# A recursive 2D filter by pairs of units: products read PSUM on VectorE, the quotient moves to GpSimd

## The chip, the cores and the metric

The kernel runs on one core of one Trainium2 chip. The metric is device time in microseconds for one launch, as the median of several runs. All data are float32.

## The reference, cut to what matters

The input `x` is (4, 512, 512, 16). Two residual layers follow each other, each on a group-normalised input. The first is a recursive filter in two dimensions that is applied by FFT; the second is a 3x3 cosine convolution. The change touches only how the filter of the first layer is built:

```python
a = jnp.pad(denumerator, ((0, 0), (0, 0), (1, 0), (1, 0)), constant_values=1.0)
b = jnp.pad(numerators, ((0, 0), (0, 0), (0, 0), (1, 0), (1, 0)), constant_values=0.0)
H_truncated = jnp.fft.rfft2(b, s=(l1, l2)) / jnp.fft.rfft2(a, s=(l1, l2))
h_truncated = jnp.fft.irfft2(H_truncated, s=(l1, l2))
H = jnp.fft.rfft2(h_truncated, s=(2 * l1, 2 * l2))
H_full = h0 + H[0]
```

`a` and `b` are 9x9 polynomials for each of 16 x 16 pairs of an input and an output channel. So for every pair of channels the kernel evaluates two complex polynomials A and B on a 512 x 257 grid, forms the complex quotient B / A = B conj(A) / |A|^2, and turns it into the spectrum of twice the size that the later convolution multiplies with.

## The kernel before, in words

Four phases run one after the other: `filter_phase` (the filter, from the weights alone, with the statistics of `x` slipped in beside it), `forward_phase` (transform of `x`), `conv_phase` (multiplication per frequency) and `last_phase` (inverse transform and second layer).

In `filter_phase` the work is a list of 1024 units: output channel j (16), column half h (2), input channel i (16, in pairs), row half kp (2). Two units that stand next to each other in the list, (i, i + 1), are a pair; there are 512. A unit covers 256 x 128 points of the grid, and passes through these steps:

- `polynomials` (L353): TensorE evaluates A and B of both units of a pair into four PSUM tiles `pab` of one bank each; in a tile the axes are partition, k (2), real or imaginary part (2), column (128). The PSUM pool `f_psab` has exactly four buffers.
- `evict` (L362, L365, L366): ScalarE (ACT) copies both tiles to SBUF (`ab`), then squares the real part of A into `sq` and the imaginary part back into PSUM.
- `square` (L370): VectorE (DVE) adds the squares to `dn`, which is |A|^2.
- `product` (L376, L377, L379): VectorE forms `m` = B A part by part and takes the reciprocal of `dn`; GpSimd (POOL) forms the crossed products `x`.
- `terms` (L383, L384): GpSimd adds and subtracts to the real and imaginary part of the numerator.
- `quotient` (L388): VectorE multiplies by the reciprocal into `sp`.
- `edge` (L393): for h = 0 ScalarE overwrites column 0 of `sp` with values `z` that `weights` has computed.
- `taps` and `placed` (L404, L415): TensorE transforms `sp` of a pair into two PSUM tiles `pg`, and ScalarE copies them into the staging tiles `st`. After the last unit of an (j, h), two `st` tiles of 4 MB each are stored in DRAM.

Beside these run three more things. `odds` (L456, L461) reads the finished part of an earlier channel back (`ev_in`), multiplies it on TensorE into `pt`, and ScalarE copies it to `ot`, which goes to DRAM; it is a generator, and each `next(rest)` copies the last `pt` and issues the matmuls of the next one. `weights` prepares the coefficients of the next channel once in 32 pairs. `quad` (L333, L335) prepares the left factors `u` of the polynomials for the next four input channels, once in four pairs; `pt` and the `pu` of `quad` share two PSUM buffers (`f_pst`). `image_stats` (L599) puts the statistics of `x` on VectorE; the scheduler places them, and `weights` and `quad` too.

All else keeps the order in which the code issues it on each of the four compute engines: the context manager `InOrder` ties each instruction to the one before it on its engine. The loop goes over units v. At v it issues `evict` and `square` for unit v, `product` for v - 1, `terms` and `quotient` for v - 2, `edge` for v - 3, and at every even v `polynomials` of the pair (v, v + 1) and `taps` and `placed` of the pair (v - 4, v - 3).

Of the kernel before, what the change touches and what calls it, by code (L numbers as in the profile page):

```python
# [40 lines left out]
F32 = mybir.dt.float32  # L41
AF = mybir.ActivationFunctionType
# [4 lines left out]
P = 128  # L47
# [154 lines left out]
def bc(ap, axis, shape):  # L202
    return ap.unsqueeze(axis).to_broadcast(shape)
# [45 lines left out]
def filter_phase(tc, cst, h0, num, den, g_d, beside):  # L249
    nc = tc.nc  # L250
    with ExitStack() as ctx:
# [3 lines left out]
        ew = ctx.enter_context(tc.tile_pool(name="f_ew", bufs=2))  # L255
# [14 lines left out]
        def weights(j):  # L270

            sa = wt.tile([18, C, 32], F32, name="sa")
            sb = wt.tile([18, C, 32], F32, name="sb")
            nc.gpsimd.dma_start(out=sa.rearrange("p i n -> p (i n)"), in_=cst["apad"])
            nc.gpsimd.memset(sb, 0.0)
            for t, src in ((sa, den), (sb, num)):
                for c in range(2):
                    nc.gpsimd.dma_start(  # L280
                        out=t[9 * c + 1 : 9 * c + 9, :, 9 * c + 1 : 9 * c + 9],
                        in_=src[:, j].rearrange("i p q -> p i q"),
                    )
            ha = sm.tile([18, C, 18], F32, name="ha")
            nc.gpsimd.tensor_mul(ha, sa[:, :, 0:18], bc(h0b[:, j :: C], 2, [18, C, 18]))
            nc.gpsimd.tensor_add(sb[:, :, 0:18], sb[:, :, 0:18], ha)


            v = sm.tile([18, 2, 4, C], F32, name="v")
            ev = sm.tile([18, 2, 2, C], F32, name="ev")  # L290
            od = sm.tile([18, 2, 2, C], F32, name="od")
            for n, t in enumerate((sa, sb)):
                for c in range(2):
                    q = 9 * c
                    nc.vector.reduce_sum(ev[:, c, n, :], t[:, :, q : q + 9 : 2], axis=AX.X)
# [24 lines left out]
            nc.vector.tensor_sub(z[:, :, 1, :], hz[:, :, 1, 0, :], hz[:, :, 0, 1, :])  # L320
            return sa, sb, z
# [19 lines left out]
        def polynomials(pair):  # L341

            for w in pair:
                w["pp"] = [ps_ab.tile([P, 2, 2, P], F32, name=f"pab{n}", tag="ab") for n in range(2)]
            for k in range(2):
                for w in pair:
                    k1 = (2 * w["kp"] + k) * P
                    for n in range(2):  # L350
                        at = 32 * (w["i"] % 4 ^ 2 * n)
                        q = slice(at, at + 18)
                        nc.tensor.matmul(  # L353
                            w["pp"][n][:, k].rearrange("p c n -> p (c n)"),
                            w["us"][n][q, k1 : k1 + P], e2[q, n, w["h"], :], start=True, stop=True,
                        )

        def evict(w):
            w["ab"] = [ew.tile([P, 2, 2, P], F32, name=f"ab{n}") for n in range(2)]
            pp = w.pop("pp")  # L360
            for n in range(2):
                nc.scalar.copy(w["ab"][n], pp[n])  # L362

            w["sq"], w["pa"] = ew.tile([P, 2, P], F32, name="sq"), pp[0]
            nc.scalar.activation(w["sq"], w["ab"][0][:, :, 0], AF.Square)  # L365
            nc.scalar.activation(pp[0][:, :, 1], w["ab"][0][:, :, 1], AF.Square)  # L366

        def square(w):
            w["dn"] = ew.tile([P, 2, P], F32, name="dn", bufs=3)
            nc.vector.tensor_add(w["dn"], w["sq"], w.pop("pa")[:, :, 1])  # L370

        def product(w):

            a, b = w["ab"]
            w["m"] = ew.tile([P, 2, 2, P], F32, name="m")
            nc.vector.tensor_mul(w["m"], b, a)  # L376
            nc.vector.reciprocal(w["dn"], w["dn"])  # L377
            w["x"] = ew.tile([P, 2, 2, P], F32, name="x", bufs=1)
            nc.gpsimd.tensor_mul(w["x"], b, a[:, :, ::-1])  # L379

        def terms(w):
            m, x = w["m"], w["x"]
            nc.gpsimd.tensor_add(m[:, :, 0], m[:, :, 0], m[:, :, 1])  # L383
            nc.gpsimd.tensor_sub(m[:, :, 1], x[:, :, 1], x[:, :, 0])  # L384

        def quotient(w):
            w["sp"] = ew.tile([P, 2, 2, P], F32, name="sp", bufs=4)
            nc.vector.tensor_mul(w["sp"], w["m"], bc(w["dn"], 2, [P, 2, 2, P]))  # L388

        def edge(w):  # L390
            if w["h"] == 0:
                kp = w["kp"]
                nc.scalar.copy(w["sp"][:, :, :, 0], w["z"][:, 2 * kp : 2 * kp + 2, :, w["i"]])  # L393
# [74 lines left out]
        def odds():  # L468

            for j in range(C):  # L470
# [4 lines left out]
        work = [dict(j=j, h=h, i=i, kp=kp)  # L475
                for j in range(C) for h in range(2) for i2 in range(0, C, 2) for kp in range(2)
                for i in (i2, i2 + 1)]
        done = [0]
        order = InOrder(tc, nc.tensor, nc.vector, nc.scalar, nc.gpsimd)
        rest = odds()  # L480
        polys = {0: weights(0)}
        us = quad(*polys[0][:2], 0)
        for v in range(len(work) + 3):
            with order:
                next(rest)
            if v % 64 == 32 and v < len(work) - 64:
                polys[v // 64 + 1] = weights(v // 64 + 1)
            first, second, third = (work[v - k] if 0 <= v - k < len(work) else None for k in (1, 2, 3))
            if third:
                with order:  # L490
                    edge(third)
            if v < len(work):
                w = work[v]
                if v % 8 == 0 and v:
                    us = ahead
                w["us"], w["z"] = us, polys[w["j"]][2]
                with order:
                    if v % 2 == 0:
                        pair = work[v : v + 2]
                        pair[1]["us"] = us  # L500
                        polynomials(pair)
            last = work[v - 4 : v - 2] if v % 2 == 0 and v >= 4 else None
            if last:
                if last[0]["i"] == 0 and last[0]["kp"] == 0:
                    st = [stp.tile([P, N, C], F32, name=f"st{a}", tag="st") for a in range(2)]
                with order:
                    pg = taps(last)
            if v < len(work):
                with order:
                    evict(work[v])  # L510
            if last:
                with order:
                    placed(last, st, pg)
                done[0] += 2
                for w in last:
                    w.clear()
            with order:
                if second:
                    terms(second)
                if first:  # L520
                    product(first)
                if second:
                    quotient(second)
                if v < len(work):
                    square(work[v])
            if v % 8 == 4 and v + 4 < len(work):
                g = (v + 4) // 8
                ahead = quad(*polys[g // 8][:2], g % 4)
            if v % 2:
                next(beside, None)  # L530
        done[0] += 8
        for _ in rest:
            pass
# [912 lines left out]
```

## Time and profile before

| | |
|---|---|
| median of 3 runs | 18399.56 us (18386.0 to 18413.88) |
| the profiled execution | 18378.82 us, its span 18377.0 us |
| mean granted TensorE clock | 0.939 |
| busy: PE, DVE, ACT, POOL | 88%, 61%, 52%, 57% of the span |
| first to last `reciprocal` of the filter (L377) | 36.6 to 5140.9 us |
| window 940 to 5140 us, busy: PE, DVE, ACT, POOL | 3617.8, 3329.4, 2513.1, 2680.0 of 4200 us |
| granted clock, 30 to 940 us and 940 to 5140 us | 0.74 and 0.89 |
| `pt` of the last channel, after the filter's units | to 5310 us |

PE is TensorE's matmul stream, PEld its weight loads. Busy is the time in which an engine executes something; a matmul's end is modelled, so a busy PE is not PE at its peak. The granted clock is the share of its full speed that TensorE was given. A row of the timeline has the start, the duration, the engine, the line of the kernel, the operation and the tiles that it writes and reads, and in brackets the idle time of the engine before it and what ended that.

### The profile page before, as it was taken

What the parts mean: (1) busy time and instruction counts of PE and PEld (TensorE: products, weight loads), DVE (VectorE), ACT (ScalarE), POOL (GpSimd) and SP (SyncE); (2) the same over time, 40 slices, a digit from 0 to 9 for tenths busy, and PEclk for the clock granted to TensorE, in tenths of its full rate; (3) what the DMA queues carried; (4) which work ended last, traced back from release to release, by engine and by line L of the source; (5) the groups of instructions that cost most, each with busy time, mean ns of one, the idle gap of its engine ahead of it and who ended that gap; (6) DMA issues with size and microseconds to landing.
All of it is one profiled execution on the core that took longest, in us unless ns stands there. A gap on an engine that the chain in (4) does not pass through costs nothing. (4 is left out here: it accounts for less than half of the span.)

```text
span 18377.0 us, 546088 instructions
## 1 busy us (share of the span) xinstructions
PE 16100.0 (88%) x233100; PEld 11615.5 (63%) x233100; DVE 11247.9 (61%) x23131; ACT 9599.6 (52%) x19919; POOL 10502.4 (57%) x10653
## 2 busy tenths in 40 slices
PE   7788888888889988888888888888888988988888
PEld 4444444444444467777777777777767776877777
DVE  8877777777833355555555555555555554246887
ACT  4556555555632255555555555555555554106788
POOL 5566666666621166666666666666666664026776
PEclk6888988888999999999999999999999999998999
DMA  4655555555676588888888888888888887795431
GB/s 123 201 162 165 162 165 162 164 163 161 167 221 184 167 319 320 318 321 324 316 321 318 319 325 323 325 325 323 323 323 314 325 320 289 257 324 192 160 129 69
DMA packets 2918877, 4543.47 MB, mean 247 GB/s; under 512 B 117634, under 2 KB 2086492, under 8 KB 2809694
## 3 DMA queue, kind: packets, MB, share of 16 engines
q1 hardware_dynamic: 2686254, 3768.39, 60.7%
q0 software_dynamic: 174896, 605.89, 8.7%
q10 hardware_dynamic: 55296, 134.24, 2.2%
q8 instruction: 1835, 30.06, 0.6%
q14 instruction: 596, 4.88, 0.1%
HBM read 3030.71 MB, written 1477.31 MB: 245 GB/s over the span
## 5 line engine op out<-in xcount | busy, mean ns | idle before, releaser
L838 PE MATMUL pg<-c_dg,g 64*128 64x128 f32 x32832 | 2836.9, 291 | 326.6 <-ACT gh L738 163.0
L854 PE MATMUL pm<-xe,gh 128*32 128x64 f32 x131328 | 2397.8, 222 | 587.8 <-issue 354.6
L854 PEld LDWEIGHTS pm<-xe,gh 128*32 128x32 f32 x131328 | 2011.9, 110 | 1165.3 <-issue 972.6
L838 PEld LDWEIGHTS pg<-c_dg,g 64*128 64x128 f32 x32832 | 2283.3, 190 | 670.4 <-issue 253.4
L456 PE MATMUL pt<-ev_in,c_todd 128*128 128x512 f32 x4096 | 2191.1, 681 | 350.4 <-ACT ot L461 323.9
L883 DVE TENSOR_TENSOR z<-zq,pz 128x256 f32<-128x256 f32 x2052 | 861.4, 420 | 2608.4 <-ACT zq L882 2531.1
L736 DVE COPY gh<-pg 128x512 f32<-128x512 f32 x2046 | 1410.1, 689 | 1312.1 <-PE pg L838 1308.2
L379 POOL TENSOR_TENSOR x<-ab,ab 128x512 f32<-128x512 f32 x1024 | 1561.1, 1524 | 1081.7 <-ACT ab L362 1029.0
L807 POOL TENSOR_TENSOR xu<-xe,c_late 128x256 f32<-128x256 f32 x2052 | 1389.5, 702 | 860.2 <-ACT xe L738 834.6
L377 DVE RECIPROCAL dn<-dn 128x256 f32<-128x256 f32 x1024 | 1781.8, 1740 | 0.0
L456 PEld LDWEIGHTS pt<-ev_in,c_todd 128*128 128x128 f32 x4096 | 792.4, 210 | 1483.1 <-issue 640.1
L738 ACT COPY yf<-pm 128x512 f32<-128x512 f32 x2046 | 1210.9, 592 | 924.0 <-PE pm L854 909.2
L362 ACT COPY ab<-pab 128x512 f32<-128x512 f32 x2048 | 1127.9, 617 | 858.7 <-PE pab L353 609.1
L818 ACT COPY xe<-xl 64x1024 f32<-64x1024 f32 x513 | 538.5, 1050 | 1872.5 <-POOL xl L809 1872.5
L738 ACT COPY gh<-pg 128x512 f32<-128x512 f32 x2058 | 1200.0, 583 | 398.4 <-PE pg L838 389.5
L875 PE MATMUL pz<-c_ident,yf 128*128 128x128 f32 x8208 | 1377.4, 291 | 30.3 <-issue 28.5
L404 PE MATMUL pg<-c_dinv,sp 64*128 64x128 f32 x16384 | 1192.7, 301 | 117.8 <-ACT sp L393 117.8
L404 PEld LDWEIGHTS pg<-c_dinv,sp 64*128 64x128 f32 x16384 | 1084.7, 209 | 313.2 <-PE pab L353 134.1
L376 DVE TENSOR_TENSOR m<-ab,ab 128x512 f32<-128x512 f32 x1024 | 1271.4, 1242 | 0.0
L809 POOL TENSOR_TENSOR xl<-xl,xu 128x1024 f32<-128x1024 f32 x513 | 1208.9, 2357 | 40.2
L383 POOL TENSOR_TENSOR m<-m 128x256 f32<-128x256 f32 x1024 | 747.0, 730 | 746.4 <-DVE m L376 746.2
L1289 PE MATMUL pc<-l_band,xn 128*128 128x160 f32 (+2 forms) x6144 | 1072.9, 333 | 53.7 <-DVE e_o L1344 53.5
(204 smaller groups left out, 31381.8 us busy)
## 6 DMA issues: line engine op xcount, KB each, us to landing
xe<-xf_d SPq DMA_DIRECT2D x1026, 1536.0 KB, 8.4
g<-g_d SPq DMA_DIRECT2D x511, 1024.0 KB, 9.8
g_d<-st SPq DMA_DIRECT2D x64, 4096.0 KB, 31.3
ev_in<-g_d SPq DMA_DIRECT2D x1024, 256.0 KB, 4.6
g_d<-ot SPq DMA_DIRECT2D x1024, 256.0 KB, 2.5
xf_d<-xe POOLq DMA_DIRECT2D x513, 448.0 KB, 8.3
xf_d<-xl POOLq DMA_DIRECT2D x513, 448.0 KB, 5.2
x_d<-xo SPq DMA_DIRECT2D x128, 1024.0 KB, 5.1
```

What stands on the lines that cost most here:

```text
L376: nc.vector.tensor_mul(w["m"], b, a)
L377: nc.vector.reciprocal(w["dn"], w["dn"])
L379: nc.gpsimd.tensor_mul(w["x"], b, a[:, :, ::-1])
L404: nc.tensor.matmul(pg[u][:, n, k].rearrange("p a x -> p (a x)"), w["sp"][q, k, c, :], dinv[q, 2 * kp + k, c, :], start=(c == 0), stop=(c = ...
L456: nc.tensor.matmul(pt, todd[:, c, kc, hh * P : hh * P + P], ev[:, kc, c], start=(kc == 0), stop=(kc == 1),)
L736: nc.vector.tensor_copy(dst, src)
L738: nc.scalar.copy(dst, src)
L807: nc.gpsimd.tensor_mul(u[:, :, h, c], xe[:, :, h, 1 - c], bc(late[:, 1 + c], 2, [P, F, 2]))
L809: nc.gpsimd.tensor_add(xl.rearrange("p f h c k -> p (f h c k)"), xl.rearrange("p f h c k -> p (f h c k)"), u.rearrange("p f h c k -> p (f ...
L838: nc.tensor.matmul(pg[c][:, j % 4], g[half, j], dg[half], start=True, stop=True)
L854: nc.tensor.matmul(pm[32 * q : 32 * q + 32, g % 8], gh[:, f].rearrange("p c j -> p (c j)"), xe[:, :, f].rearrange("p t h c k -> p t (h c k ...
L875: nc.tensor.transpose(pz[:, t % 4].rearrange("p v q x -> p (v q x)"), y[:, at].rearrange("p g x -> p (g x)"), ident)
```

## The change

The loop goes over pairs p instead of units. In an iteration `last` is the pair p - 2, `mid` is p - 1 and `new` is p. ScalarE copies only A to SBUF (`a`), and squares straight from PSUM. VectorE forms both kinds of products, `m` and `x`, out of B's PSUM tile, and adds `dn`; the two reciprocals of a pair come after all its products and after the `polynomials` and `evict` of the new pair in the code. GpSimd does `terms` and the `quotient`. `taps` of a pair stands before `polynomials` of the new one, and `next(rest)` is called at the start of an iteration and ahead of `evict`. Some SBUF buffers grow in number (`a`, `sq`, `m`, `dn` to 4, `x` to 3). The number of PSUM buffers is the same.

```diff
         def evict(w):
-            w["ab"] = [ew.tile([P, 2, 2, P], F32, name=f"ab{n}") for n in range(2)]
-            pp = w.pop("pp")
-            for n in range(2):
-                nc.scalar.copy(w["ab"][n], pp[n])
-
-            w["sq"], w["pa"] = ew.tile([P, 2, P], F32, name="sq"), pp[0]
-            nc.scalar.activation(w["sq"], w["ab"][0][:, :, 0], AF.Square)
-            nc.scalar.activation(pp[0][:, :, 1], w["ab"][0][:, :, 1], AF.Square)
-
-        def square(w):
-            w["dn"] = ew.tile([P, 2, P], F32, name="dn", bufs=3)
-            nc.vector.tensor_add(w["dn"], w["sq"], w.pop("pa")[:, :, 1])
-
-        def product(w):
-
-            a, b = w["ab"]
-            w["m"] = ew.tile([P, 2, 2, P], F32, name="m")
-            nc.vector.tensor_mul(w["m"], b, a)
-            nc.vector.reciprocal(w["dn"], w["dn"])
-            w["x"] = ew.tile([P, 2, 2, P], F32, name="x", bufs=1)
-            nc.gpsimd.tensor_mul(w["x"], b, a[:, :, ::-1])
+            pa, _ = w["pp"]
+            w["a"] = ew.tile([P, 2, 2, P], F32, name="a", bufs=4)
+            nc.scalar.copy(w["a"], pa)
+            w["sq"] = ew.tile([P, 2, P], F32, name="sq", bufs=4)
+            nc.scalar.activation(w["sq"], pa[:, :, 0], AF.Square)
+            nc.scalar.activation(pa[:, :, 1], pa[:, :, 1], AF.Square)
+
+        def products(w):
+
+            (pa, pb), a = w.pop("pp"), w["a"]
+            w["m"] = ew.tile([P, 2, 2, P], F32, name="m", bufs=4)
+            nc.vector.tensor_mul(w["m"], pb, a)
+            w["x"] = ew.tile([P, 2, 2, P], F32, name="x", bufs=3)
+            nc.vector.tensor_mul(w["x"], pb, a[:, :, ::-1])
+            w["dn"] = ew.tile([P, 2, P], F32, name="dn", bufs=4)
+            nc.vector.tensor_add(w["dn"], w["sq"], pa[:, :, 1])
...
         def quotient(w):
             w["sp"] = ew.tile([P, 2, 2, P], F32, name="sp", bufs=4)
-            nc.vector.tensor_mul(w["sp"], w["m"], bc(w["dn"], 2, [P, 2, 2, P]))
+            nc.gpsimd.tensor_mul(w["sp"], w["m"], bc(w["dn"], 2, [P, 2, 2, P]))
...
+        for p in range(n_pairs + 2):
+            new, mid, last = (work[2 * (p - k) : 2 * (p - k) + 2] if 0 <= p - k < n_pairs else [] for k in range(3))
             with order:
                 next(rest)
...
             if last:
...
+                    for w in last:
+                        edge(w)
+                    placed(last, st, taps(last))
...
             with order:
-                if second:
-                    terms(second)
-                if first:
-                    product(first)
-                if second:
-                    quotient(second)
-                if v < len(work):
-                    square(work[v])
...
+                for w in mid:
+                    products(w)
+                    terms(w)
+            if new:
...
+                with order:
+                    polynomials(new)
+            with order:
+                next(rest)
+                for w in new:
+                    evict(w)
+                for w in mid:
+                    nc.vector.reciprocal(w["dn"], w["dn"])
+                    quotient(w)
+            if p % 4 == 2 and p + 2 < n_pairs:
+                g = (p + 2) // 4
+                ahead = quad(*polys[g // 8][:2], g % 4)
+            next(beside, None)
```

In the changed kernel's own numbering the lines are: `a` L361, squares L363 and L364, `m` L370, `x` L372, `dn` L374, `terms` L378 and L379, `quotient` L383, `edge` L388, `taps` L399, `placed` L410, reciprocal L511, `pt` L451, `ot` L456.

More of the change, by code (lines that the diff above doesn't have):

```diff
@@ L482, in filter_phase @@
         us = quad(*polys[0][:2], 0)
-        for v in range(len(work) + 3):
+        n_pairs = len(work) // 2
+        for p in range(n_pairs + 2):
+            new, mid, last = (work[2 * (p - k) : 2 * (p - k) + 2] if 0 <= p - k < n_pairs else [] for k in range(3))
             with order:
                 next(rest)
[L486 to L491, printed above, removed]
-            if v < len(work):
[L493 to L502, printed above, removed]
+            if p % 32 == 16 and p < n_pairs - 32:
+                polys[p // 32 + 1] = weights(p // 32 + 1)
             if last:
@@ L506, in filter_phase @@
                 with order:
[L507 to L513, printed above, removed]
+                    for w in last:
+                        edge(w)
+                    placed(last, st, taps(last))
                 done[0] += 2
@@ L517, in filter_phase @@
             with order:
-                if second:
-                    terms(second)
-                if first:
-                    product(first)
-                if second:
-                    quotient(second)
-                if v < len(work):
-                    square(work[v])
-            if v % 8 == 4 and v + 4 < len(work):
-                g = (v + 4) // 8
+                for w in mid:
+                    products(w)
+                    terms(w)
+            if new:
+                if p % 4 == 0 and p:
+                    us = ahead
+                for w in new:
+                    w["us"], w["z"] = us, polys[w["j"]][2]
+                with order:
+                    polynomials(new)
+            with order:
+                next(rest)
+                for w in new:
+                    evict(w)
[4 more added lines that the diff above has]
+                g = (p + 2) // 4
                 ahead = quad(*polys[g // 8][:2], g % 4)
-            if v % 2:
-                next(beside, None)
+            next(beside, None)
         done[0] += 8
```

## The prediction, made before the changed kernel had run

> **What bounds the kernel now.** I read the windows first, to see which stretch the change can reach, then the timeline of an undisturbed pair of units, engine by engine, then what disturbs pairs, then rows for operations that are new. The filter runs from 30 to 5140 us of an 18377.0 us span; what follows keeps its order, so a gain there moves the end one for one. VectorE near 5130 us (start, us, engine, line):
>
> ```profile
> 5127.60 0.40 DVE L370 TENSOR_TENSOR dn<-sq,pab 128x256 f32<-128x256 f32 x1
> 5127.93 1.43 DVE L376 TENSOR_TENSOR m<-ab,ab 128x512 f32<-128x512 f32 x1
> 5129.28 1.74 DVE L377 RECIPROCAL dn<-dn 128x256 f32<-128x256 f32 x1
> 5130.95 0.62 DVE L388 TENSOR_TENSOR sp<-m,dn 128x512 f32<-128x512 f32 x1
> 5131.49 0.40 DVE L370 TENSOR_TENSOR dn<-sq,pab 128x256 f32<-128x256 f32 x1
> ```
>
> No idle time stands behind a row: from `dn` to the next `dn` is 3.89, a unit, and the starts of L377, every second one, give 7.76 for a pair. Records overlap their successors by 0.08, so the starts give each step's share: `dn` 0.33, `m` 1.35, reciprocal 1.67, `sp` 0.54. PE in the same pair:
>
> ```profile
> 5127.23 3.83 PE L456 MATMUL pt<-ev_in,c_todd 128*128 128x512 f32 x8
> 5130.99 0.71 PE L353 MATMUL pab<-c_e,u 18*128 18x256 f32 x6
> 5131.95 1.13 PE L353 MATMUL pab<-c_e,u 18*128 18x256 f32 x10 [0.25 <-DVE dn L370]
> 5133.00 2.06 PE L404 MATMUL pg<-c_dinv,sp 64*128 64x128 f32 x32
> ```
>
> It idles only 0.25 of the 7.76. And with `quad`, once in four pairs:
>
> ```profile
> 2413.19 1.06 PE L333 MATMUL pu<-c_e,sa 18*32 18x512 f32 x8
> 2415.03 1.06 PE L333 MATMUL pu<-c_e,sb 18*32 18x512 f32 x8 [0.78 <-ACT ot L461]
> 2416.02 3.70 PE L456 MATMUL pt<-ev_in,c_todd 128*128 128x512 f32 x8
> 2419.65 1.15 PE L353 MATMUL pab<-c_e,u 18*128 18x256 f32 x16
> 2420.73 2.06 PE L404 MATMUL pg<-c_dinv,sp 64*128 64x128 f32 x32
> 2422.71 3.83 PE L456 MATMUL pt<-ev_in,c_todd 128*128 128x512 f32 x8
> ```
>
> `quad` costs PE 2.83 (2413.19 to 2416.02). Then `pab` comes in one piece, 1.08, and the pair takes 6.69. With `pt` at 3.75 and `pg` at 1.98, PE's own work is 6.81: VectorE is the bound by less than 1 us.
>
> The starts of L377 give all pairs. The first 80, with the image statistics beside them, take 904 us: 76 at 10.3 and four near 31. The other 431 take 4196: 282 at 7.76, 27 at 29.1, 122 between, so 404 undisturbed ones of 8.44 on average. Two windows show what disturbs (columns: PE, PEld, DVE, ACT, POOL busy, clock, DMA share, GB/s):
>
> ```profile
> 2060.00:2080.00 20.00, 8.49 (x53) 5.15 (x54) 4.54 (x6) 5.75 (x17) 3.98 (x4) 0.67 0.99 267
> 2448.00:2450.00 2.00, 2.00 (x7) 0.79 (x4) 1.88 (x3) 1.76 (x5) 1.84 (x3) 0.58 0.44 131
> ```
>
> In the first the store of two `st` tiles fills the DMA engines and all engines stand. The second lies behind the next `quad`: after 74 of 107 quads the trace has the granted clock halved, mostly for 3.41 us, in which PE loses 1.71.
>
> **The change part by part**, for a pair.
>
> *Products (L370, L372 of the changed kernel).* VectorE loses two `m` (2 x 1.35) and two `sp` (2 x 0.54) and gets four 128x512 products with an operand in PSUM. The nearest row is the cosine of the last phase, PSUM times SBUF in the same shape (ns, least/median/most); below it the old `m`:
>
> ```profile
> L1307 DVE TENSOR_TENSOR e_y<-pc,l_rin x256: 627/684/701, 16647.6 to 18359.8; 128x512 f32<-128x512 f32 x128
> ```
> ```profile
> L376 DVE TENSOR_TENSOR m<-ab,ab x1024: 672/1418/1873, 35.7 to 5139.6; 128x512 f32<-128x512 f32 x171
> ```
>
> Bounds 0.63 and 1.42; I take 0.68, pitch 0.60, for its operands lie as the new ones do, and `m` shows what slows it: at its least it takes 0.67, and 1.43 where GpSimd's `x` (1.64) runs beside it, while `dn`, PSUM and SBUF, stays at 0.40 beside that `x`. VectorE: 4 x 0.60 + 2 x 0.33 + 2 x 1.67 = 6.40 (7.02 with no overlap) against 7.76. The Trainium skill (GPSIMD Engine Reference, Specifications) says that GpSimd shares its SBUF interfaces with VectorE, with contention when VectorE reads two SBUF inputs. The trace's `m` agrees; by that rule none of VectorE's new work is slowed.
>
> *Quotient on GpSimd (L383).* It loses two `x` and gets two 128x512 products. Bounds: 1.06 (L1330, two broadcast inputs) and 1.64; I take 1.28 (L1335, same shape, 1.26 to 1.31). GpSimd: 4 x 0.73 + 2 x 1.28 = 5.5, at worst 6.2, under PE's 6.81. The second `sp` is ready 1.3 after its reciprocal; `pg` (L399) asks for it an iteration later.
>
> *B is not evicted.* The order of instructions has 1,024 ACT copies fewer, 0.48 each by their starts. ACT has idle time, so that saves nothing; its squares read PSUM instead of SBUF, 0.38 to 0.49 by the rows, nothing either way. What goes is cover. All four `pab` buffers belong to one pair, and B's two now wait for a VectorE product. ACT's starts in the pair:
>
> ```profile
> 5128.39 0.63 ACT L461 COPY ot<-pt 128x512 f32<-128x512 f32 x1
> 5128.87 1.14 ACT L362 COPY ab<-pab 128x512 f32<-128x512 f32 x2
> 5129.82 0.49 ACT L365 ACTIVATE sq<-ab 128x256 f32<-128x256 f32 x1
> 5130.14 0.45 ACT L366 ACTIVATE pab<-ab 128x256 f32<-128x256 f32 x1
> ```
>
> `ot` 0.48, a copy 0.48, squares 0.32. PE now runs `pt`, `pg` of pair p-2, `pab` of p, `pt`. Laid out from `pab` at 0: `pt` from 1.08 to 2.95, next `pt` to 4.83, `pg` to 6.81. ACT first ends four `st` copies and `ot`, so `a` starts at 1.8; the reciprocals of p-1 end at 2.0, the products run from 2.5 to 5.6, and `pab` of p+1 wants them at 6.81: 1.2 to spare. Were they later, `pt` and `pg` would queue behind `pab`. For h = 0 `pg` also waits for `edge`, on ACT behind `ot`. That loop is `st` 1.06, `ot` 0.48, evict 2 x 1.12, `ot` 0.48, edges 0.24, `pg` 1.98, and five hand-overs of 0.08 (`m` ends at 5129.36, GpSimd starts at 5129.44): 6.88. So PE becomes the bound, at 6.81 to 6.88.
>
> *Reciprocals last.* They lie beside `pab` and evict, as laid out. The queues of SP, ACT and GpSimd issue the same DMAs in nearly the same order. The statistics end some 16 units later in VectorE's order, at no cost.
>
> *quad and storms.* `quad` will wait for an `ot` behind evict; by the layout its halves start 1.84 apart, as now, so 2.83 again, but on the engine that bounds. The store of `st` is DMA time: nothing saved.
>
> **Sum.** Four later pairs take 4 x 6.83 + 2.83 + (74/107) x 1.71 = 31.3, or 7.83 each, and 0.13 for `weights` (4 us a channel, 13 channels, 404 pairs): 7.96 against 8.44, x 404 = 194 us. First 80: VectorE gives 1.36, or 0.74 without overlap, with PE partly in the way at a clock of 0.74; I take 0.9 x 76 = 68. Together 262. The profiled execution took 18378.82, 1.82 around its span, and would go to 18117; the median of the runs is 20.7 above it, 18399.56 - 262 = 18138, say 18140.
>
> **The rivals.** *The same (10%): a serial loop through ACT.* With whole durations instead of starts the h = 0 loop is 1.21 + 0.63 + 2 x 1.5 + 0.63 + 0.50 + 2.06 + 0.4 = 8.4. Half of the pairs then cost 8.4 + 0.71 + 0.30 + 0.13 = 9.5, or +222; the other half saves 97, the first pairs 68: 18457 at the full price, 18400 at three quarters of it, which I take. Against it: ACT's rows do overlap. *Slower (9%): the products cost what `m` did.* VectorE then takes 4 x 1.35 + 0.66 + 3.34 = 9.40 and hides `quad`: +1.09 x 404 and +1.6 x 76, 18960. It decides from a pitch of 1.08: 4 x 1.08 + 4.0 = 8.31 = 8.44 - 0.13. For it: part of `m`'s 1.42 might not be GpSimd's doing; against it L1307. *Slower (6%): the clock.* If PE's pauses before `pab` halve the clock in each pair, 6.83 + 1.71 + 0.71 + 0.13 = 9.38, +380, 18780. Against it: from 2400 to 2500 us no stretch of 3.41 us in which PE was busy for over 90% has a halved clock behind it, and PE will idle less. The Trainium skill (TensorE: Matmul & The Clock Gate, A second HAM failure mode: psum-queue depth-cycling) tells of a kernel whose clock swings because PE pauses as it cycles through PSUM; the trace has that only behind quads and storms.
>
> **How the numbers follow.** Forecast 75%, rivals 25%. No change means within 0.2%, 37 us, about what a measurement of this kernel can tell. Low end: no halved clock, 7.52 + 0.13, 0.79 x 404 = 319, and 1.4 x 76 = 106: 17974, say 17970. High end: PE keeps its 0.25 of waits, each quad halves the clock, the first pairs give nothing: (4 x 7.08 + 2.83 + 1.71)/4 + 0.13 = 8.34, 40 us, 18360; to take in most of the serial loop, 18420. The other two, 15%, lie beyond. Faster 0.75, same 0.09, slower 0.16.
>
> **What would show it.** Right: L370 and L372 near 0.68, L383 near 1.28, pairs by the starts of L511 at 6.8 to 7.0, PE all but never idle between quads. Wrong: products over 1.08; `pab` waiting for `dn` or `x` for over 0.5 a pair; `pg` waiting for `edge`; a mean clock under 0.85 from 1000 us to the filter's end.

## The result, and the profile after

The changed kernel takes 18162.74 us (median of 4 runs, 18159.94 to 18203.43) against 18398.17 for the kernel before beside it: 235 us less, a ratio of 0.9877 with a 95% interval of 0.986 to 0.9894. The forecast was 18140 in a range of 17970 to 18420. Its profiled execution has a span of 18157.8 us against 18377.0, and the 219 us between them lie in the filter: its reciprocals run from 39.9 to 4923.3 us; in the kernel before they ran from 36.6 to 5140.9.

The timeline of VectorE in an undisturbed pair and the start of the next (start, us, engine, line, operation, tiles, shapes, count, then idle time before the row and who ended it; `...` stands for rows left out, here and in the code):

```profile
2616.32 0.69 DVE L370 TENSOR_TENSOR m<-pab,a 128x512 f32<-128x512 f32 x1 [0.80 <-ACT a L361]
2616.93 0.68 DVE L372 TENSOR_TENSOR x<-pab,a 128x512 f32<-128x512 f32 x1
2617.52 0.41 DVE L374 TENSOR_TENSOR dn<-sq,pab 128x256 f32<-128x256 f32 x1
2617.85 0.68 DVE L370 TENSOR_TENSOR m<-pab,a 128x512 f32<-128x512 f32 x1
...
2619.38 3.35 DVE L511 RECIPROCAL dn<-dn 128x256 f32<-128x256 f32 x2
2623.11 0.69 DVE L370 TENSOR_TENSOR m<-pab,a 128x512 f32<-128x512 f32 x1 [0.37 <-ACT a L361]
```

A pair now takes 2623.11 - 2616.32 = 6.79 us instead of 7.76, and VectorE, which had no idle time, waits 0.37 in it for `a`. TensorE, which idled 0.25 us in the pair before, is now the one without a gap:

```profile
2618.75 2.06 PE L399 MATMUL pg<-c_dinv,sp 64*128 64x128 f32 x32
2620.74 1.15 PE L353 MATMUL pab<-c_e,u 18*128 18x256 f32 x16
2621.81 3.70 PE L451 MATMUL pt<-ev_in,c_todd 128*128 128x512 f32 x8
2625.54 2.06 PE L399 MATMUL pg<-c_dinv,sp 64*128 64x128 f32 x32
...
2630.52 1.06 PE L333 MATMUL pu<-c_e,sa 18*32 18x512 f32 x8
2632.24 1.06 PE L333 MATMUL pu<-c_e,sb 18*32 18x512 f32 x8 [0.66 <-ACT ot L456]
```

`quad`, the last two rows, waits as it did: its second half stands until `ot` is copied, 0.66 here against 0.78 before. The new operations, each by its own line (ns, least/median/most):

```profile
L370 DVE TENSOR_TENSOR m<-pab,a x1024: 615/683/694, 34.9 to 4920.1; 128x512 f32<-128x512 f32 x171
...
L372 DVE TENSOR_TENSOR x<-pab,a x1024: 665/679/686, 35.5 to 4920.7; 128x512 f32<-128x512 f32 x171
...
L383 POOL TENSOR_TENSOR sp<-m,dn x1024: 1257/1272/1319, 41.7 to 4925.2; 128x512 f32<-128x512 f32 x171
```

The first 80 pairs, with the statistics beside them, are another matter: 904 us before, 897 after. There VectorE and ScalarE hold each other up. From the waits of the changed kernel between 380 and 930 us (who waited <- for whom: total us, times, longest):

```profile
DVE stats L585 <- DMA xs<-in_x: 98.3, 32, 10.5
...
ACT pab L364 <- DVE stats L585: 66.0, 32, 8.1
...
ACT a L361 <- DVE stats L585: 49.1, 15, 7.2
...
ACT st L410 <- DVE stats L585: 22.8, 3, 9.0
```

The same rows of the kernel before, in the same window:

```profile
DVE stats L599 <- DMA xs<-in_x: 49.7, 18, 6.5
...
ACT u L335 <- DVE stats L599: 6.1, 1, 6.1
...
ACT st L415 <- DVE stats L599: 4.1, 2, 2.4
```

So ScalarE stood 138 us for the statistics, where it had stood 10, and VectorE's wait for the loads of `xs` doubled.

Nothing in `evict` reads the statistics. The timeline of both engines in the changed kernel shows what ScalarE stands at:

```profile
600.85 1.06 DVE L585 BATCH_NORM_STATS2 stats<-xs 128x6 f32<-128x128 f32 x5 [1.09 <-DMA xs<-in_x]
...
602.15 3.36 DVE L511 RECIPROCAL dn<-dn 128x256 f32<-128x256 f32 x2
...
604.04 0.39 ACT L363 ACTIVATE sq<-pab 128x256 f32<-128x256 f32 x1
...
605.43 1.19 DVE L585 BATCH_NORM_STATS2 stats<-xs 128x6 f32<-128x128 f32 x6
...
606.08 0.33 ACTq L573 DMA_DIRECT2D xs<-in_x  x1
...
606.46 0.37 ACT L364 ACTIVATE pab<-pab 128x256 f32<-128x256 f32 x1 [2.02 <-DVE stats L585]
```

ScalarE has done `sq` at 604.43 and comes to the load of the next `xs` tile in its own queue (L573). There are two `xs` buffers, and the load may not go out before VectorE has finished the statistics of the tile that holds its buffer; these stand behind both reciprocals in VectorE's order. So ScalarE's square of the same unit, and the evict after it, come 2.02 later, and VectorE's products with them.

### The profile page after: what moved, and what is told of

Read it like the earlier page. It is cut to its first block, busy times and chain, and to the rows that moved or that the text cites. A ratio compares the mean times of both kernels' runs of the same rounds, so it can differ in the third digit from the quotient of the medians.

```text
span 18157.8 us, 546802 instructions
## 1 busy us (share of the span) xinstructions
PE 15836.8 (87%) x233100; PEld 11492.6 (63%) x233100; DVE 10706.4 (59%) x23131; ACT 9126.2 (50%) x18895; POOL 10230.0 (56%) x10653
## 5 line engine op out<-in xcount | busy, mean ns | idle before, releaser
L451 PE MATMUL pt<-ev_in,c_todd 128*128 128x512 f32 x4096 | 2110.2, 658 | 93.0 <-ACT ot L456 70.6
L511 DVE RECIPROCAL dn<-dn 128x256 f32<-128x256 f32 x1024 | 1717.7, 1717 | 0.0
L383 POOL TENSOR_TENSOR sp<-m,dn 128x512 f32<-128x512 f32 x1024 | 1302.6, 1272 | 643.5 <-DVE dn L511 593.8
L451 PEld LDWEIGHTS pt<-ev_in,c_todd 128*128 128x128 f32 x4096 | 782.0, 204 | 1166.1 <-issue 779.2
L410 ACT COPY st<-pg 128x256 f32<-128x256 f32 x2048 | 620.1, 390 | 1736.3 <-PE pg L399 1272.6
L399 PEld LDWEIGHTS pg<-c_dinv,sp 64*128 64x128 f32 x16384 | 1059.9, 205 | 663.4 <-ACT sp L388 352.6
L378 POOL TENSOR_TENSOR m<-m 128x256 f32<-128x256 f32 x1024 | 746.1, 729 | 1244.8 <-DVE m L370 1244.2
L399 PE MATMUL pg<-c_dinv,sp 64*128 64x128 f32 x16384 | 1162.4, 296 | 215.6 <-ACT sp L388 178.6
L370 DVE TENSOR_TENSOR m<-pab,a 128x512 f32<-128x512 f32 x1024 | 698.3, 682 | 1084.2 <-ACT a L361 1051.1
```

The costliest lines, as they stand in the source:

```text
L383: nc.gpsimd.tensor_mul(w["sp"], w["m"], bc(w["dn"], 2, [P, 2, 2, P]))
L399: nc.tensor.matmul(pg[u][:, n, k].rearrange("p a x -> p (a x)"), w["sp"][q, k, c, :], dinv[q, 2 * kp + k, c, :], start=(c == 0), stop=(c = ...
L451: nc.tensor.matmul(pt, todd[:, c, kc, hh * P : hh * P + P], ev[:, kc, c], start=(kc == 0), stop=(kc == 1),)
```

## The experiments

There were three groups of four; the kernel before, run beside each, took 18398.24, 18350.69 and 18337.83 us, so kernels of different groups are compared by their ratio to it (0.0010 is 18 us). Most intervals are 0.0009 to 0.0017 to each side. Stages come from the traces, by the starts of the reciprocals: the sums over the first 80 pairs and over the other 431. A storm is the three pairs around a store of `st`. "h = 0" and "h = 1" are the median pair of each half of a channel without `quad` and clear of the storms and of `weights` (12 of each 32 pairs); "quad" is the mean pair with `quad` that is clear of the same.

| kernel | ratio to before | first 80 | other 431 | h = 0 | h = 1 | quad |
|---|---|---|---|---|---|---|
| before | 1 | 904 | 4196 | 7.76 | 7.76 | 9.69 |
| changed | 0.9877 | 897 | 3985 | 6.79 | 6.69 | 10.40 |
| `xs` on SyncE | 0.9843 | 791 | 4031 | 6.79 | 6.69 | 10.40 |
| statistics in order | 0.9768 | 701 | 4015 | 6.79 | 6.69 | 10.36 |
| the same in before | 0.9945 | 775 | 4228 | 7.77 | 7.77 | 9.81 |
| half of `pt` | 0.9811 | 878 | 3895 | 6.79 | 6.27 | 10.06 |
| half of `pt`, edge on GpSimd | 0.9718 | 760 | 3833 | 6.27 | 6.27 | 9.86 |
| two SBUF inputs | 1.0032 | 932 | 4239 | 8.09 | 8.09 | 9.38 |
| quotient on VectorE | 0.9983 | 907 | 4146 | 7.97 | 7.97 | 8.24 |
| reciprocals by unit | 0.9910 | 908 | 4038 | 6.79 | 6.98 | 10.01 |
| units | 0.9962 | 897 | 4116 | 7.17 | 7.08 | 10.38 |
| statistics in order, `pu` in `pg`'s buffers | 0.9723 | 687 | 3921 | 6.79 | 6.69 | 8.89 |
| the same and edge on GpSimd | 0.9678 | 666 | 3851 | 6.69 | 6.69 | 8.88 |

**The first 80 pairs.** The theory is the loop just shown. The first test takes the loads off ScalarE's queue.

```diff
-        nc.scalar.dma_start(out=t, in_=x[b, ...])
+        nc.sync.dma_start(out=t, in_=x[b, ...])
```

> The changed kernel, with the loads of the image statistics (xs, L573) issued by SyncE instead of ScalarE. Theory (a loop through two queues holds the first 80 pairs): ScalarE stands before each load until VectorE has finished the statistics of the tile that held the buffer, and these lie behind reciprocals in VectorE's order; then evict is late and VectorE waits for a. With the loads off ScalarE's queue its waits for stats go (by the waits of 380 to 930 us: 66 us at L364, 49 at L361, 23 at L410), and the first 80 pairs fall from 897 us to 830 to 860: the whole by 40 to 65 us, to 18100 to 18120. Rival (VectorE's own work, 6.40 + 2.95 a pair, or the loads' transfer bounds this stretch): 880 us or more, the whole within 15 us of the changed kernel. The other 431 pairs stay at 3985 by both.

18107.52 us (18088.91 to 18126.98, 5 runs), 0.9843 (0.983 to 0.9857): 55 under the changed kernel's median (by the ratios 0.0034, give or take 0.0022), and the trace's 511 pairs add up to 60 less (4881.7 to 4822.0). In its list of waits from 380 to 930 us no row has ScalarE waiting for `stats` any more; the rows that stand there now for the evict's copy and for the loads are

```profile
ACT a L361 <- PE pab L353: 45.8, 25, 5.9
...
DVE stats L585 <- DMA xs<-in_x: 19.0, 3, 16.4
```

So most loads also come in time (19.0 instead of 98.3). The first 80 pairs fell by more than expected, 106, and the other 431 rose by 46, where none was expected: of pairs over 20 us there are two fewer in the first part and two more in the second, so part of this is where the line between the parts happens to lie, and the sum is the sounder number. The Trainium skill (DMA: Bandwidth & Descriptors, Issuing engines are not separate DMA queues) says that DMAs run on the same engines whoever issues them, and that spreading them only saves the issuing time, usually small. Here ScalarE lost more to a load than its issue: an issue takes 0.33 us of its queue, 43 for all 128 loads, and the waits in front of the issues were 138 us in this window alone. The edit takes both off ScalarE, and this run does not tell apart what each was worth. SyncE now does the waiting, 207.7 us for `stats` in the same window, with the stores of `ot` and the loads of `ev_in` behind it; that cost less.

The second test leaves the loads on ScalarE, and ties the statistics to the loop, two in each pair, instead of letting them run ahead.

```diff
-            next(beside, None)
+            with order:
+                next(beside, None)
```

> The changed kernel, with the image statistics held to the order of the loop: two bn_stats in every pair over all 511 pairs, instead of about 12 in each of the first 80. Theory (VectorE has slack once PE is the bound): the first 80 pairs cost what the later ones do on average (3984.5 / 431 = 9.25 us, so 740 instead of 897), and the later ones pay only what the 0.47 us of statistics a pair does not find idle on VectorE, 0.05 to 0.3 us: +20 to +120. Together 40 to 140 us less; I take 110, 18050. Rival (VectorE is as full as it was): the work costs the same wherever it stands, 404 x 0.47 = 190 more against 157 less, so 18160 to 18200.

17980.56 us (17947.61 to 17996.32, 4 runs), 0.9768 (0.9755 to 0.9782): 182 under the changed kernel, more than the 40 to 140. The first 80 pairs cost 701 (740 expected), the others 31 more (20 to 120 expected). The median pair stays at 6.79, though the first of every four in h = 0 rises to 6.95, with this on VectorE:

```profile
2575.85 0.42 DVE L586 BATCH_NORM_STATS2 stats<-xs 128x6 f32<-128x128 f32 x2
...
2576.18 0.67 DVE L370 TENSOR_TENSOR m<-pab,a 128x512 f32<-128x512 f32 x1
```

In the pair shown the statistics stand where VectorE waited 0.37 for `a`, and no wait is left there. The control was the same edit in the kernel before.

> The same edit in the kernel before, as a control. Theory (there VectorE was the bound, with no slack in 300 of the 404 undisturbed pairs): first 80 pairs 125 us less (9.74 x 80 = 779 instead of 904), the others 300 x 0.47 = 140 more: within 40 us of the kernel before, 18360 to 18440. Rival (the early stretch loses its time to ScalarE's queue in both kernels, so that spreading the statistics helps both alike): 40 to 140 us less than before here too.

18301.83 us (18277.26 to 18331.3, 5 runs), 0.9945 (0.9933 to 0.9958): 96 us less, so this expectation missed, and the rival's number came. Not for the rival's reason, though: the kernel before hardly lost time to ScalarE's queue (the 10 us above), and its first 80 pairs fell by 129, about the theory's 125. It was the later pairs, which were to pay 140 on a full VectorE, that paid only 32, and their median stays at 7.77. VectorE in this run, with GpSimd's `x` (POOL, L379) put in:

```profile
2598.42 1.65 POOL L379 TENSOR_TENSOR x<-ab,ab 128x512 f32<-128x512 f32 x1
...
2599.18 1.43 DVE L376 TENSOR_TENSOR m<-ab,ab 128x512 f32<-128x512 f32 x1
2600.53 1.74 DVE L377 RECIPROCAL dn<-dn 128x256 f32<-128x256 f32 x1
...
2602.31 1.64 POOL L379 TENSOR_TENSOR x<-ab,ab 128x512 f32<-128x512 f32 x1
...
2603.07 0.47 DVE L600 BATCH_NORM_STATS2 stats<-xs 128x6 f32<-128x128 f32 x2
2603.46 1.03 DVE L376 TENSOR_TENSOR m<-ab,ab 128x512 f32<-128x512 f32 x1
...
2606.94 1.43 DVE L376 TENSOR_TENSOR m<-ab,ab 128x512 f32<-128x512 f32 x1
```

From the first `m` to the last it is 7.76, as without statistics. Behind them `m` starts 0.39 later and takes 1.03 instead of 1.43. Both times it ends 0.54 after GpSimd's `x` does (2600.61 and 2600.07, 2604.49 and 2603.95), and that is the rule: in the kernel before, of 749 `m` between 960 and 4800 us that start while `x` runs, 98% end 0.546 to 0.554 after it, whenever they started. So `m` stood until `x` was done and then ran: 0.89 of its 1.43 was a wait. A VectorE without a gap did have room: it was busy waiting, inside `m`. Moving the statistics was worth 96 us in the kernel before and 182 after the change; the other 86 are there only with the change. By the traces it is 69, nearly all of it in the first 80 pairs (197 less against 129).

**What bounds an undisturbed pair now.** Half of each `pt` is left out, which takes 1.87 us a pair from TensorE.

```diff
-                        for kc in range(2):
+                        for kc in range(1):
                             nc.tensor.matmul(
...
-                                start=(kc == 0), stop=(kc == 1),
+                                start=True, stop=True,
                             )
```

> The changed kernel, with the second of the two accumulating matmuls of every pt left out (its output is not the reference's): PE loses 4 x 0.47 = 1.87 us a pair, from 6.81 to 4.94. Theory (PE bounds the undisturbed pair): the median pair falls from 6.79 us to what VectorE takes, 6.40 to 6.55, and quad hides, so that the 404 later pairs fall from 7.86 on average to 6.6 to 7.0: 350 to 500 us less, 17650 to 17800. Rival 1 (VectorE bounds it, at 6.8 with waits between): the median stays at 6.75 to 6.8 and only quads gain, 250 us at most. Rival 2 (the edge loop through ScalarE bounds pairs of h = 0): those stay at 6.79 and the pairs of h = 1 fall to 6.4 to 6.55.

18050.97 us (18041.04 to 18075.78, 4 runs), 0.9811 (0.9797 to 0.9824): 112 less, not 350 to 500. By the pairs it is rival 2: those of h = 1 fall from 6.69 to 6.27 (the rival had 6.4 to 6.55), those of h = 0 stay at 6.79. TensorE in one of these:

```profile
2611.57 1.98 PE L451 MATMUL pt<-ev_in,c_todd 128*128 128x512 f32 x4
2615.30 2.06 PE L399 MATMUL pg<-c_dinv,sp 64*128 64x128 f32 x32 [1.75 <-ACT sp L388]
```

TensorE is done early, and `pg` then waits for `edge`, which stands in ScalarE's order behind `st`, `ot`, both evicts and `ot`. Nor did `quad` hide, as the theory had it (10.06 against 10.40): its second `pu` still waits for `ot`, a median of 1.08 us instead of 0.66, and the granted clock is halved behind 69 of 107 quads instead of 43. The next run takes `edge` out of that loop, on top of the same edit: GpSimd does it, behind its quotient.

```diff
-                nc.scalar.copy(w["sp"][:, :, :, 0], w["z"][...])
+                nc.gpsimd.tensor_copy(w["sp"][:, :, :, 0], w["z"][...])
...
                 with order:
-                    for w in last:
-                        edge(w)
                     placed(last, st, taps(last))
...
                     quotient(w)
+                    edge(w)
```

> As the run with half of each pt left out (0.9811 of before; its pairs of h = 0 took 6.79 us, those of h = 1 took 6.3), with edge on GpSimd right behind the quotient instead of on ScalarE behind ot; the output is not the reference's. Theory (the loop st, ot, evict, ot, edge, pg holds the pairs of h = 0): they fall to 6.3 to 6.4 as well, 60 to 90 us less, 0.976 to 0.978 of before. Rival (ScalarE's list or GpSimd's holds them): they stay at 6.75 to 6.8, 0.980 to 0.982.

17817.74 us (17797.79 to 17830.57, 4 runs), 0.9718 (0.9703 to 0.9732). All undisturbed pairs are at 6.27, and no row of VectorE in them has idle time before it, so the loop through `edge` is what held h = 0, and VectorE holds both halves now. The gain is larger than expected because the first 80 pairs fall too, by 118; the later ones fall by 62, as expected. Why the first ones do was not tested by itself.

So three limits lie close together: VectorE at 6.27, TensorE at 6.69, the loop through `edge` at 6.79.

**The parts of the change.** First the operands: A twice from SBUF, where the changed kernel reads B from PSUM.

```diff
-            nc.vector.tensor_mul(w["m"], pb, a)
+            nc.vector.tensor_mul(w["m"], a, a)
...
-            nc.vector.tensor_mul(w["x"], pb, a[:, :, ::-1])
+            nc.vector.tensor_mul(w["x"], a, a[:, :, ::-1])
```

> The changed kernel, but the four products of a pair read A twice from SBUF (a times a) instead of B in PSUM and A in SBUF; the output is not the reference's. Theory (two SBUF inputs on VectorE are slowed while GpSimd works, as m was before): L370 and L372 rise from 0.68 us to 1.0 to 1.42, VectorE's pair from 6.40 to 4 x (0.92 to 1.34) + 4.0 = 7.7 to 9.4; the median pair goes from 6.79 to at least 7.6, the whole up by 300 to 700 us, 18460 to 18860. Rival (m's 1.42 was its own): both stay at 0.68, and the whole within 30 us of the changed kernel.

18417.98 us (18394.11 to 18426.14, 7 runs), 1.0032 (1.0021 to 1.0044): slower than the kernel before, and 0.0155 over the changed kernel, 285 us, just under the expected 300. VectorE and GpSimd in one stretch:

```profile
2601.30 0.62 DVE L370 TENSOR_TENSOR m<-a 128x512 f32<-128x512 f32 x1
2601.85 1.75 DVE L372 TENSOR_TENSOR x<-a 128x512 f32<-128x512 f32 x1
...
2603.00 1.18 POOL L378 TENSOR_TENSOR m<-m 128x256 f32<-128x256 f32 x1
```

A product of the same shape takes 0.62 where it starts with GpSimd idle and 1.75 where it starts in the middle of a GpSimd operation (medians: 0.71 for L370, under the 1.0 that was expected at least, and 1.21 for L372); GpSimd's L378 takes 1.18 instead of 0.73 (the median of the changed kernel). The pair is 8.09. The Trainium skill (SBUF — State Buffer, Who interferes with whom) says that a VectorE instruction with two SBUF inputs contends with a GpSimd instruction that reads SBUF, and one with a single SBUF input doesn't. Both halves agree: 0.68 with B in PSUM, 1.75 without in the row shown.

The quotient, put back on VectorE:

```diff
-            nc.gpsimd.tensor_mul(w["sp"], w["m"], bc(w["dn"], ...))
+            nc.vector.tensor_mul(w["sp"], w["m"], bc(w["dn"], ...))
```

> The changed kernel with the quotient back on VectorE (nothing else moved). Theory: VectorE gets 2 x 0.54 more a pair, 6.40 + 1.08 = 7.48, and bounds the pair again: the median pair goes from 6.79 us to 7.3 to 7.5, some 300 undisturbed pairs without quad pay 0.5 to 0.7 each, and the others little: 120 to 230 us more than the changed kernel, 18280 to 18390. Rival (VectorE has that much room, so the quotient's move brought nothing): median at 6.8, within 30 us of the changed kernel.

18313.13 us (18299.91 to 18345.69, 10 runs), 0.9983 (0.9974 to 0.9992): 0.0106 over the changed kernel, 195 us, as expected. The pair is longer than expected, 7.97:

```profile
2604.91 1.75 DVE L511 RECIPROCAL dn<-dn 128x256 f32<-128x256 f32 x1
2606.76 0.69 DVE L383 TENSOR_TENSOR sp<-m,dn 128x512 f32<-128x512 f32 x1
2607.37 1.75 DVE L511 RECIPROCAL dn<-dn 128x256 f32<-128x256 f32 x1
2609.22 0.69 DVE L383 TENSOR_TENSOR sp<-m,dn 128x512 f32<-128x512 f32 x1
```

Here `sp` reads the reciprocal right in front of it and starts 1.85 after that one's start, not 1.67 as behind another unit's reciprocal in the kernel before. Part of it comes back where `quad` is hidden again (8.24).

The place of the reciprocals: each right behind its unit's `dn` (moved from the end of the pair into `products`).

```diff
             nc.vector.tensor_add(w["dn"], w["sq"], pa[:, :, 1])
+            nc.vector.reciprocal(w["dn"], w["dn"])
...
-                    nc.vector.reciprocal(w["dn"], w["dn"])
                     quotient(w)
```

> The changed kernel with each reciprocal behind its own unit's dn, instead of both at the end of the pair. Theory (the last place lets both units' products give their PSUM back before the reciprocals): the second unit's dn comes 1.67 us later, pab of the next pair was to have 1.2 to spare, so PE waits 0.3 to 0.5 a pair: the median pair goes from 6.79 to 7.1 to 7.3, the whole up by 100 to 200 us, 18260 to 18360. Rival (the order within VectorE does not matter): within 30 us of the changed kernel, pairs at 6.8.

18181.37 us (18168.46 to 18214.95, 4 runs), 0.9910 (0.9893 to 0.9926): 0.0033 over the changed kernel, 60 us give or take 43, less than the 100 to 200 expected. VectorE and TensorE:

```profile
2601.12 1.75 DVE L375 RECIPROCAL dn<-dn 128x256 f32<-128x256 f32 x1
...
2602.79 0.63 DVE L370 TENSOR_TENSOR m<-pab,a 128x512 f32<-128x512 f32 x1
...
2603.79 1.73 PE L353 MATMUL pab<-c_e,u 18*128 18x256 f32 x16
```

The mechanism is there: the second unit's products start behind the reciprocal, and `pab` is stretched from 1.15 to 1.73 as it waits for them. But it strikes only some of the pairs: the median is 7.19 over all 431 later ones, 6.79 over the undisturbed ones of h = 0 and 6.98 over those of h = 1, which lie on both sides of that number.

Last, the new operations in the old loop over single units (products ahead of `pab`, reciprocal and quotient behind `evict`, one unit an iteration; the diff to the kernel before, cut to the loop):

```diff
+            if first:
+                with order:
+                    products(first)
+                    terms(first)
...
-                if second:
-                    terms(second)
                 if first:
-                    product(first)
-                if second:
-                    quotient(second)
-                if v < len(work):
-                    square(work[v])
+                    nc.vector.reciprocal(first["dn"], first["dn"])
+                    quotient(first)
```

> The new operations in the old loop over single units: products of B in PSUM by VectorE, quotient by GpSimd, B not evicted, but one unit an iteration, its products ahead of pab, its reciprocal and quotient behind evict. Theory (the gain comes from VectorE's shorter list, the order is worth some tenths a pair at most): 135 to 235 us under the kernel before, the median pair 6.8 to 7.2. Rival (the pairs carry the gain, since only they let PE and ScalarE run ahead of VectorE): less than 100 us under before, a median pair over 7.4.

18256.21 us (18251.36 to 18282.57, 5 runs), 0.9962 (0.9948 to 0.9976): 82 us under before. Neither expectation holds whole: the median pair, 7.17, is the theory's, the sum is the rival's. A pair gains 0.6 of the 1.0 that the changed kernel gains, and a pair with `quad` costs what it does in the changed kernel (10.38): the other 431 pairs fall by 80 instead of 212. So the new operations in the old loop brought about a third of the change's gain (0.0038 of 0.0123 by the ratios). The rest came with the loop over pairs, which also places `edge`, `taps`, `placed` and `next(rest)` otherwise; which of these it was is open.

**`quad` and the clock.** On top of the statistics in order, `pu` gets the two PSUM buffers of `pg`, which are free once `st` is copied, so it need not wait for `ot`.

```diff
-                pu = ps_t.tile([P, N], F32, name=f"pu{n}", tag="t")
+                pu = ps_g.tile([P, N], F32, name=f"pu{n}", tag="pg")
```

> The kernel with the statistics in the loop's order (17981 us), and quad's pu in the two PSUM buffers of pg instead of the two of pt. Theory (on PE, which has no room, quad costs 0.7 us more than its 2.12 because the second pu waits for ot, and its pauses bring part of the halved clocks): a pair with quad falls from 9.6 us by 0.7, 128 times, 90 us; with half of the halved clocks gone (41 of 107 quads, 1.71 each) 40 more: 17850 to 17900. Rival (the wait moves: the next pg now waits for u's copies, which stand behind evict and ot on ScalarE): within 30 us of 17981.

17838.07 us (17821.01 to 17873.55, 5 runs), 0.9723 (0.9706 to 0.9739) against 0.9768: 83 us less, give or take 39, where 90 to 130 were expected. TensorE at `quad`:

```profile
2591.16 1.98 PE L451 MATMUL pt<-ev_in,c_todd 128*128 128x512 f32 x4
2593.07 1.06 PE L333 MATMUL pu<-c_e,sa 18*32 18x512 f32 x8
2593.95 1.04 PE L333 MATMUL pu<-c_e,sb 18*32 18x512 f32 x8
2594.92 1.99 PE L451 MATMUL pt<-ev_in,c_todd 128*128 128x512 f32 x4
```

No pause is left, and the granted clock is halved behind none of the 107 quads, where it was behind 41 of them with the statistics in order and 43 in the changed kernel. A pair with `quad` falls from 10.36 to 8.89, by more than the 0.7 of the wait. `quad` itself takes TensorE 1.85 in the rows shown (2593.07 to 2594.92), against 2.71 in the changed kernel (2630.52 to 2633.23).

**A version that beats both.** The move of `edge` to GpSimd, with the diff shown above, is added to that.

> Statistics in the loop's order, pu in pg's buffers (together 0.9723 of before) and edge on GpSimd. Theory (both PE at 6.7 and the edge loop at 6.79 hold pairs of h = 0): their median goes from 6.79 to 6.95 us to 6.7, 0.1 to 0.25 in 130 pairs, and 20 to 40 us go: 0.970 to 0.9712 of before. Rival (PE alone holds them, or GpSimd's edge is late): 0.9715 or more.

17743.55 us (17736.01 to 17749.01, 4 runs), 0.9678 (0.9663 to 0.9692), the fastest kernel of this study, 594 us under the kernel before. The pairs of h = 0 go to 6.69, as the theory has it; 83 us instead of 20 to 40, as the three pairs around a storm also fall, from 45.7 to 43.6 us in all. A last edit splits the loads of `sa` and `sb` off `weights` and issues them six pairs earlier in the program.

```diff
+            if p % 32 == 10 and p < n_pairs - 32:
+                got = loads(p // 32 + 1)
             if p % 32 == 16 and p < n_pairs - 32:
-                polys[p // 32 + 1] = weights(p // 32 + 1)
+                polys[p // 32 + 1] = weights(p // 32 + 1, *got)
```

> The same, with the loads of sa and sb for the next channel six pairs ahead of the work on them. Theory (in the pair with weights, 15.1 us against 12.95 in the kernel before, VectorE stands 6 us at the sums of sa, behind a DMA that was just issued): that pair falls to 10 to 12, in 15 channels 45 to 75 us less than the last one. Rival (its chain of divide and pz holds the pair): within 20 us of it.

17759.09 us (17746.61 to 17760.76, 4 runs), 0.9685 (0.9671 to 0.9699): no difference. It settles nothing on `weights`, for the trace shows the loads where they were: the first of a channel, which GpSimd issues, at 2219.82 us instead of 2220.28. The edit had not moved them in GpSimd's order.

## Why the prediction was right, and where not

*Products.* Right in size and reason: 0.68, pitch 0.60, as for the cosine's row; the run with two SBUF inputs shows that the old `m` was slow because of GpSimd. The rival "the products cost what `m` did" falls with it.

*Quotient.* 1.27 against 1.28.

*VectorE's pair.* 6.40 forecast; 6.27 where nothing else holds it. Of the 1.49 that VectorE's list lost (7.76 to 6.27), 0.97 to 1.07 arrived.

*TensorE becomes the bound, 6.81 to 6.88.* 6.69 for h = 1, and 6.79 for h = 0, where the loop through `edge` holds, which the prediction laid out at 6.88. That both limits were there and so close is shown by the two runs with half of `pt`, and by the 6.69 of the last version, which has `edge` on GpSimd and `pt` whole. The serial loop rival, at 8.4, took whole durations where the rows overlap.

*`quad` and the halved clock.* 6.83 + 2.83 + (74/107) x 1.71 = 10.84 forecast, 10.40 measured, with 43 of 107 halved instead of 74. `quad` itself took TensorE 2.71 instead of the 2.83. It did lose its cover: it cost 9.69 - 7.76 = 1.93 over the mean undisturbed pair before and 10.40 - 6.74 = 3.66 after. The rival of a clock that is halved in each pair did not come (the mean is 0.90 between 940 and 4905 us). The Trainium skill (TensorE: Matmul & The Clock Gate, A second HAM failure mode: psum-queue depth-cycling) tells of a clock that swings because TensorE pauses as it cycles through PSUM. Away from storms and `weights`, this trace has halved clocks only behind `quad`, and the run in which `pu` need not wait for a buffer has 0 of 107 of them.

*Weights and storms.* A storm's three pairs take 45.2 against 45.4 us: nothing saved, as said. The three pairs around `weights` exceed undisturbed ones by 8.0 us instead of 5.2, where the prediction took 4 and no change.

*The 431 later pairs.* 194 forecast, 212 measured: regular pairs 0.09 shorter than assumed (27 us over the 297 without `quad` that the sum counted), quads 0.44 shorter (47 over 107), against 2.8 us in each of 13 channels for `weights` (36); some 20 us are not placed.

*The first 80 pairs: the step that failed.* "First 80: VectorE gives 1.36, or 0.74 without overlap [...] I take 0.9 x 76 = 68." Measured: 7. The step took VectorE's shorter list as the gain and named TensorE's clock as the only thing in the way. What it costed at nothing in the part on the reciprocals ("The statistics end some 16 units later in VectorE's order, at no cost") sits in a loop: load of `xs` in ScalarE's queue, statistics in VectorE's, evict behind the load. ScalarE's waits for the statistics went from 10 to 138 us between 380 and 930 us, and VectorE, with a shorter list, idled 121 us there instead of 88, above all for `xs`. Taking the loads off that queue gives 60 us back over all pairs, about the 61 that were missing. That the total came near is luck in part: of the profiled executions' 219 us against 262, the first pairs brought 61 less than forecast and the later ones 18 more.

## What to carry to other kernels

A DMA that waits for a buffer holds up everything behind it in its issuer's queue: ask who frees the buffer, where that stands in its engine's order, and what stands behind the load in the queue that issues it. SyncE waited longer than ScalarE had, and what stood behind it there was less urgent. When the bound moves by one engine, lay out the next two limits as well; here three lay within about 0.5 us, and work that the old bound had covered (`quad`, 83 us) and room that the old bound now had (for the statistics, 182 us) were together worth as much as the change itself. An engine without idle time may still have room, where one of its instructions stands waiting for a neighbour inside its own duration.

## What the runs showed of the hardware that was not expected

- A VectorE product with two SBUF inputs that starts while GpSimd works does not run slower, it waits: it ends 0.55 after GpSimd's operation does, whether it started 0.49 or 0.89 before that end. It goes both ways: in the run with two SBUF inputs, 773 of GpSimd's L378 between 960 and 4800 us start inside a VectorE product, and 98% of them end 0.58 to 0.59 after it. The wait is counted into the duration of the row (1.75 against 0.62 and 1.18 against 0.73 in the rows shown).
- On VectorE, an instruction that reads the result of the one right in front of it started 1.85 us after that reciprocal's start, not 1.67: 0.18 of overlap is lost. Likewise a reciprocal started 0.44 after its own `dn` (2600.68 to 2601.12, reciprocals by unit), and 0.33 after another unit's (2619.05 to 2619.38, changed).
- A pause between the halves of `quad` goes with a granted clock that is halved afterwards in some of the cases: 74 of 107 with a median pause of 0.78 us (before), 43 with 0.66 (changed), 69 with 1.08 (half of `pt`), none without the pause. What decides which quads it strikes is open: in the kernel before, the pauses with and without a halved clock behind them have the same median, 0.78. That the pause alone does it is not shown, as the edit that took it away also moved `pu` to other buffers.
